# Cross-attention with 32 batches on one core: the context's values with channels stationary and 512 tokens moving, and a new order of fill and end

## The chip, the cores and the metric

One core of a Trainium2 chip runs the whole kernel. The metric is the time of one execution on the device in microseconds (us), lower is better. A core has five engines with an instruction queue each: TensorE (PE in the profile; its weight loads have a row of their own, PEld), VectorE (DVE), ScalarE (ACT), GpSimd (POOL) and SyncE (SP). SP issues all DMA transfers of this kernel, in order, and 16 DMA engines carry them out. Each engine works through its own queue in order, and semaphores make it wait for the others.

## The reference

```python
# x: (32, 512, 640) f32; ctx: (32, 77, 1024) f32; 20 heads of 32 channels
q = heads(x @ to_q_w)                       # to_q_w: 640 x 640
h_txt = sdpa(q, heads(ctx @ to_k_w), heads(ctx @ to_v_w))   # 1024 x 640 each
# the "object", "others" and "ip" parts attend to slices [77:81], [81:85], [85:] of the
# context, which has 77 rows: these slices are empty and add nothing
out = merge(h_txt) @ to_out_w + to_out_b + x
# sdpa(q, k, v) = softmax(q @ k.T / sqrt(32)) @ v, per batch and head
```

Everything is in float32. The kernel keeps that precision by splitting an operand into a high part that TensorE can take and a low part, the difference, and by adding three products (high x high, high x low, low x high: the list PAIRS).

## The kernel before, in words

**Fill.** The 32 x 77 = 2464 rows of the context are treated as one list of tokens, cut into five groups (GROUPS_KV): four of 512 and one of 416. For each group `context` (L139) loads the rows on SP, transposes them on VectorE so that channels lie on partitions, and `split` (L103: the high part by a copy on ACT, the low part by a subtraction on VectorE) makes the eight tiles `ct` (nine buffers). `keys` (L167) multiplies them with the key weights for five blocks j of 128 channels (keys stationary on the weight side, 512 tokens moving, 24 matmuls a block) and stores the split result `ks` to the scratch tensor k_dram. `context_values` (L191) does the values the other way round: 128 tokens of the context are stationary, 320 channels of the value weights (half h of 640) move. Its result is already [tokens, channels]; it is split into `vs` and stored, 640 KB and one DMA for 128 tokens, to v_dram, laid out [token, head, channel, high/low]. Group 0 also loads and splits the key weights (wk, inside `context`) and then the value weights (wv); group 1 is followed by the query weights (wq) and group 2 by the output weights, which are split and parked in wo_dram. `kvc` holds three buffers of raw context (`cs`). In the last group x of batch 0 is loaded, transposed and split.

Up to L289 the order of instructions on each engine comes from a planner: a program order serves as priority, and the planner simulates when each instruction could start. After that, under `manual_schedule`, each engine's order is the program's.

**Slots.** The main part has N = 160 slots, one for each batch b and channel block j (four heads each). `slot(n)` (L568) contains: `scores(n, t)` for the four blocks t of 128 queries (PE, then a maximum on VectorE), `exps` (ACT), the queries of slot n + 1 (`queries`, PE; `split_q`, ACT and VectorE), and the softmax of slot n - 1: `sums` (VectorE), `normalize` (POOL), `transpose_p` (32 x 32 transposes on VectorE, then four stores to a scratch tensor `pd`), and the load back as `raw` (`load_p`). Three slots later (LAG = 3) `cast_p` (ACT), `rest_p` (ACT and VectorE) and `last_p` (POOL) split these probabilities into `pp`, and `values` (PE) and `split_a` follow (`take` is both). `piece` issues the output projection of an earlier batch in portions of four steps (12 matmuls of 320 columns); `finish` adds the projection to the residual `xr` on VectorE, which frees the `po` bank, and stores a finished block of 128 rows. There are three po banks. A slot has output pieces from n = 7 on (`has_out`). `refill` reloads keys and values of the next batch from k_dram and v_dram (`load_keys`, `load_values`).

**Between fill and slots.** The values of the last group are computed in the manual part, as eight halves on a pool of three PSUM banks (`psv`): four ahead of slot 0, two in slot 0 and two in slot 1. Then the pools of the fill are released, `load_p(0)` follows, and the split output weights come back from wo_dram in five loads of 640 KB: two after slot 2, two after slot 3, one after slot 4.

**End.** `end` (L638) completes slots 157 to 159 and the output of the last two batches.

## Time and profile before

| | |
|---|---|
| median of 3 runs | 1980.47 us (1978.42 to 1981.48) |
| profiled execution: time / span | 1980.38 / 1978.6 us |
| mean granted TensorE clock | 0.991 |
| busy: PE, PEld | 1946.0 us (98%), 1761.7 us (89%) |
| busy: ACT, DVE, POOL | 1595.6 us (81%), 1345.8 us (68%), 986.0 us (50%) |
| DMA queue of SP | 555,789 packets, 421.1 MB, 83.8% of 16 engines |

The span goes from the first to the last instruction; the profiled execution's own time is 1.8 us longer. Busy shares are averages over fill, slots and end, which have different limits; a stage is to be read on its own. "PE" counts a matmul as busy from its issue to its modelled end, so matmuls overlap and a mean duration is longer than the distance from one to the next. A wait is put down to the semaphore that came last.

### The profile page before, as it was taken

What the parts mean: (1) busy time and instruction counts of PE and PEld (TensorE: products, weight loads), DVE (VectorE), ACT (ScalarE), POOL (GpSimd) and SP (SyncE); (2) the same over time, 40 slices, a digit from 0 to 9 for tenths busy, and PEclk for the clock granted to TensorE, in tenths of its full rate; (3) what the DMA queues carried; (4) which work ended last, traced back from release to release, by engine and by line L of the source; (5) the groups of instructions that cost most, each with busy time, mean ns of one, the idle gap of its engine ahead of it and who ended that gap; (6) DMA issues with size and microseconds to landing.
All of it is one profiled execution on the core that took longest, in us unless ns stands there. A gap on an engine that the chain in (4) does not pass through costs nothing.

```text
span 1978.6 us, 38192 instructions
## 1 busy us (share of the span) xinstructions
PE 1946.0 (98%) x11012; PEld 1761.7 (89%) x11012; DVE 1345.8 (68%) x2156; ACT 1595.6 (81%) x6377; POOL 986.0 (50%) x620
## 2 busy tenths in 40 slices
PE   9999998999999999999999999999999999999998
PEld 7889996799999999999999999999999999999997
DVE  4443235777777777777777777777777777777763
ACT  3322137899999999999999999999999999999982
POOL 0000033566555555565555666655665556655644
PEclk9999999899999999999999999999999999999999
DMA  7994368888889898889888988888888888888975
GB/s 170 217 263 120 96 146 206 212 220 228 228 220 229 224 225 230 225 231 225 228 223 225 226 229 221 234 223 228 226 227 226 225 224 219 225 228 225 231 195 156
DMA packets 555996, 423.54 MB, mean 214 GB/s; under 512 B 170191, under 2 KB 459501, under 8 KB 555789
## 3 DMA queue, kind: packets, MB, share of 16 engines
q1 hardware_dynamic: 555789, 421.10, 83.8%
q8 instruction: 91, 1.49, 0.3%
q14 instruction: 116, 0.95, 0.2%
HBM read 245.61 MB, written 175.32 MB: 213 GB/s over the span
## 4 chain that ended last, share of the span: by engine, by line
PE 90%; DMA 4%; SPq 2%; ACT 1%; DVE 1%; issue 1%; POOL 1%; DVEq 0%; ACTq 0%; POOLq 0%
PE po L503 28%; PE pq L346 28%; PE pa L473 15%; PE sc L381 10%; PE pv L200 4%; PE pk L171 4%; DMA raw<-pd 1%; SPq L114 1%; DMA k_dram<-ks 1%; SPq L155 1%; DMA v_dram<-vs 1%; DMA wraw<-in_L_xattn_to_k_w_dram 0%; POOL pn L414 0%; DMA wraw<-in_L_xattn_to_out_w_dram 0%; DMA cs<-in_ctx_dram 0%
## 5 line engine op out<-in xcount | busy, mean ns | idle before, releaser
L399 ACT ACTIVATE pn<-sc,nm 128x77 f32<-128x77 f32 x2560 | 797.6, 328 | 44.6 <-DVE nm L389 31.1
L414 POOL TENSOR_TENSOR pn<-pn,rs 128x1232 f32<-128x1232 f32 x160 | 364.3, 2277 | 670.2 <-DVE rs L409 655.4
L503 PE MATMUL po<-wo_s,at 128*128 128x320 f32 x3840 | 626.9, 312 | 3.0 <-DVE xr L531 3.0
L346 PE MATMUL pq<-xt,wq_s 128*128 128x512 f32 x2400 | 621.0, 399 | 0.0
L503 PEld LDWEIGHTS po<-wo_s,at 128*128 128x128 f32 x3840 | 566.3, 189 | 3.6 <-DVE xr L531 3.2
L399 ACT ACTIVATION_READ_ACCUMULATOR pn<-sc,nm 128x1 f32 x2560 | 529.3, 207 | 0.0
L389 DVE TENSOR_REDUCE nm<-sc 128x4 f32<-128x308 f32 x640 | 294.5, 460 | 335.0 <-PE sc L381 330.6
L346 PEld LDWEIGHTS pq<-xt,wq_s 128*128 128x128 f32 x2400 | 430.4, 190 | 76.7
L473 PE MATMUL pa<-pp,vb 128*128 128x512 f32 x1280 | 331.2, 400 | 13.0 <-POOL pp L459 11.0
L238 POOL TENSOR_TENSOR xt<-xs,xt 128x512 fp32r<-128x512 f32 x160 | 203.9, 1292 | 269.2 <-ACT xt L237 262.0
L473 PEld LDWEIGHTS pa<-pp,vb 128*128 128x128 f32 x1280 | 243.3, 197 | 53.7 <-POOL pp L459 13.5
L421 DVE STREAM_TRANSPOSE z<-pn 128x1280 f32<-128x1280 f32 x160 | 241.0, 1506 | 21.4 <-POOL pn L414 19.7
L452 DVE TENSOR_TENSOR pp<-raw,pp 128x1024 fp32r<-128x1024 f32 x160 | 196.2, 1226 | 59.5 <-ACT pp L445 52.8
L381 PEld LDWEIGHTS sc<-kc,qt 128*128 128x128 f32 x1280 | 213.0, 190 | 23.6 <-issue 2.1
L381 PE MATMUL sc<-kc,qt 128*128 128x154 f32 x1280 | 223.1, 256 | 2.4 <-DVE qt L363 2.3
L459 POOL TENSOR_TENSOR pp<-raw,pp 64x512 fp32r<-64x512 f32 x160 | 208.7, 1305 | 27.0 <-ACT pp L451 14.6
L363 DVE TENSOR_TENSOR qt<-pq,qt 64x512 fp32r<-64x512 f32 x320 | 214.2, 669 | 6.9 <-ACT qt L357 2.5
L496 POOL TENSOR_TENSOR xr<-xr,bias 128x640 f32<-128x640 f32 x128 | 200.8, 1570 | 9.7
L361 ACT CAST qt<-qt 64x512 fp32r<-64x512 f32 x320 | 198.1, 619 | 9.0
L381 PE MATMUL sc<-kb,qt 128*128 128x308 f32 x640 | 195.9, 306 | 0.0
L445 ACT CAST pp<-raw 128x1024 fp32r<-128x1024 f32 x160 | 170.1, 1063 | 9.3 <-DMA raw<-pd 9.2
L104 ACT CAST at<-pa 128x512 fp32r<-128x512 f32 x160 | 94.5, 591 | 94.8 <-PE pa L473 94.7
(40 smaller groups left out, 1528.5 us busy)
## 6 DMA issues: line engine op xcount, KB each, us to landing
pd<-z SPq DMA_DIRECT2D x640, 160.0 KB, 3.5
raw<-pd SPq DMA_DIRECT2D x160, 512.0 KB, 4.5
xs<-in_x_dram SPq DMA_DIRECT2D x128, 320.0 KB, 6.1
xr<-in_x_dram SPq DMA_DIRECT2D x128, 320.0 KB, 3.9
out_dram<-xr SPq DMA_DIRECT2D x128, 320.0 KB, 3.0
raw<-pd SPq DMA_DIRECT2D x160, 128.0 KB, 4.4
v_dram<-vs SPq DMA_DIRECT2D x19, 640.0 KB, 3.7
k_dram<-ks SPq DMA_DIRECT2D x80, 128.0 KB, 2.4
```

The costliest lines, as they stand in the source:

```text
L238: low.tensor_tensor(parts[1], src, parts[0].bitcast(F32), ALU.subtract)
L346: nc.tensor.matmul(pqs[n], wq_s[:, k, a, j * P : (j + 1) * P], xts[b, k][:, c, :], start=(k == 0 and m == 0), stop=(k == NC_ - 1 and m == 2),)
L363: nc.vector.tensor_tensor(qt[r, 1 + w, :], pq[r], qt[r, 0, :].bitcast(F32), ALU.subtract)
L381: nc.tensor.matmul(sc[:, cols], qt[:, m, t * P : (t + 1) * P], keys_, start=(m == 0), stop=(m == 2),)
L389: nc.vector.tensor_reduce(nm, sc[:, :KCOLS].rearrange("p (h k) -> p h k", k=NKEY), AX.X, ALU.max, negate=True)
L399: nc.scalar.activation(pnb[n % 2][:, at, :NKEY], sc[:, i * NKEY : (i + 1) * NKEY], AF.Exp, bias=nm[:, i : i + 1], accum_out=sms[n][:, at : ...
L414: nc.gpsimd.tensor_tensor(pf, pf, rs.unsqueeze(2).to_broadcast([P, NQ * HPC, NKEY]), ALU.mult)
L421: nc.vector.transpose(z.rearrange("p b t j -> p t b j"), pn.rearrange("p (t h) k -> p t (h k)", t=NQ).rearrange("p t (b i) -> p t b i", i=Q),)
L459: nc.gpsimd.tensor_tensor(pp[64:, 4, :], raw[:64, 2, :], pp[:64, 4, :].bitcast(F32), ALU.subtract)
L473: nc.tensor.matmul(pas[n], vb[:, t, :, a], pp[:, c, :], start=(m == 0), stop=(m == len(PASSES) - 1),)
L496: nc.gpsimd.tensor_tensor(xrs[b, t], xrs[b, t], bias, ALU.add)
L503: nc.tensor.matmul(pos[b, t, h][:, :HALF], ats[b * NC_ + j][:, a, t * P : (t + 1) * P], wos[0][:, j, c, h * HALF : (h + 1) * HALF], start= ...
```

## The change

1. **Values of the context.** `context_values(g0, gn, j, pool)` now works on a block j of 128 channels: the value weights are stationary, the group's tokens (512 or 416) move, 24 matmuls a block. The result is [channels, tokens]; VectorE transposes it in 32 x 32 blocks out of PSUM into `vt`, it is split from there into `vs`, and four DMAs (one for each of the four heads of the block) store it. v_dram is laid out [token, head in block, block, channel, high/low], so that one store writes pieces of 256 bytes, and `load_values` reads pieces of two or three blocks.
2. **Context a group ahead.** Loading is a function of its own, `load_context`; the loads of group g + 1 are written after the split of group g and ahead of its keys. The store of zeros comes after the first group's loads, and a context load ahead of the key weights of the same k.
3. **Keys.** Groups 0 to 3 run k outside and j inside; only the last group has j outside.
4. **Last group's values.** Five blocks in place of eight halves: two ahead of slot 0, one in slot 0, two in slot 1.
5. **Slots without output pieces (n < 7).** `last_p` comes ahead of `normalize`; `transpose_p` comes after `split_q` and `exps(n, 2)`; `scores(n, 3)` comes ahead of `values`. The five loads of the output weights follow slots 2 to 6, one each.
6. **Last slot and end.** In slot 159 both pieces come ahead of `values(156)`, and its score blocks are not held up by them. In `end`, the pieces 6 and 7 of the batch before come with a `finish` each ahead of `transpose_p(159)`; the last batch's output blocks are closed two by two with the start of the last one between; the very last block is stored in two halves.

```diff
-    v_dram = dram.tile([NT + KPAD - NKEY, HEADS, HD, 2], FPR, name="v_dram")
+    v_dram = dram.tile([NT + KPAD - NKEY, HPC, NC_, HD, 2], FPR, name="v_dram")
...
+    def load_context(g0, gn, k0, kn):
         src = ehs_flat[g0 : g0 + gn, :].rearrange("(a j) (q u) -> q j a u", j=Q, q=4)
...
+        cs = kvc.tile([P, G // Q, 4 * Q], F32, tag="cs", name="cs", bufs=3)
+        for q in range(4):
+            nc.sync.dma_start(
+                cs[q * Q : (q + 1) * Q, : gn // Q, : kn * Q],
+                src[q, :, :, k0 * Q : (k0 + kn) * Q],
+            )
+        for k in range(kn):
+            css[g0, k0 + k] = cs[:, : gn // Q, k * Q : (k + 1) * Q]
+
+    def context(g0, gn, k):
+        raw = kvt.tile([P, G], F32, tag="craw", name="craw")
+        nc.vector.transpose(
+            raw[:, :gn].rearrange("p (a j) -> p a j", j=Q), css.pop((g0, k))
+        )
+        ct = kvp.tile([P, 2, G], FPR, tag="ct", name="ct", bufs=9)
+        split(ct[:, 0, :gn], ct[:, 1, :gn], raw[:, :gn])
+        cts.append(ct)
...
+    def context_values(g0, gn, j, pool):
+        na = gn // Q
         pv = pool.tile([P, G], F32, tag="ps", name="pv")
         for k in range(NK):
             for n, (a, c) in enumerate(PAIRS):
                 nc.tensor.matmul(
-                    pv[:tn, :HALF],
-                    cts[k][:, a, t0 : t0 + tn],
-                    wv_s[:, k, c, h * HALF : (h + 1) * HALF],
+                    pv[:, :gn],
+                    wv_s[:, k, a, j * P : (j + 1) * P],
+                    cts[k][:, c, :gn],
                     start=(k == 0 and n == 0),
                     stop=(k == NK - 1 and n == 2),
                 )
...
+        vt = kvp.tile([P, G], F32, tag="vt", name="vt", bufs=1)
+        nc.vector.transpose(vt[:, :gn], pv[:, :gn])
+        vs = kvp.tile([P, G // Q, HD, 2], FPR, tag="vs", name="vs", bufs=2)
+        split(vs[:, :na, :, 0], vs[:, :na, :, 1], vt[:, :gn].rearrange("p (a d) -> p a d", d=HD))
+        dst = v_dram[g0 : g0 + gn, :, j].rearrange("(a t) i d c -> i t a (d c)", t=Q)
+        for i in range(HPC):
             nc.sync.dma_start(
-                v_dram[g0 + t0 : g0 + t0 + tn].rearrange("p h d a -> p (h d a)").bitcast(F32),
-                vs[:tn].rearrange("p h d a -> p (h d a)").bitcast(F32),
+                dst[i].bitcast(F32),
+                vs[i * Q : (i + 1) * Q, :na].rearrange("p a d c -> p a (d c)").bitcast(F32),
             )
...
-    for g0, gn in GROUPS_KV:
-        context(g0, gn)
-        if g0 == GROUPS_KV[-1][0]:
+    g0, gn = GROUPS_KV[0]
+    starts = {0: 1, 1: 1, 2: 2, 4: 4}
+    for k in range(NK):
+        if k in starts:
+            load_context(g0, gn, k, starts[k])
+        split_weights(wk_s[:, k], wk, k)
+        context(g0, gn, k)
...
+    for g, (g0, gn) in enumerate(GROUPS_KV):
+        if g:
+            cts.clear()
+            for k in range(NK):
+                context(g0, gn, k)
+        if g + 1 < len(GROUPS_KV):
+            for k0 in range(0, NK, 4):
+                load_context(*GROUPS_KV[g + 1], k0, 4)
+        else:
...
-        if g0 == 0:
+        if g + 1 < len(GROUPS_KV):
             for k in range(NK):
                 for j in range(NC_):
                     keys(g0, gn, j, k)
...
-            for t0 in range(0, gn, P):
-                for h in range(2):
-                    context_values(g0, gn, t0, h, psk)
+            for j in range(NC_):
+                context_values(g0, gn, j, psk)
...
-        v = v_dram.rearrange("n (j i) d a -> n j i (d a)", i=HPC)
+        v = v_dram.rearrange("n i j d a -> n j i (d a)")
...
-            if h == 1:
+            if (b, t) == (B - 1, NQ - 1):
+                nc.sync.dma_start(out[b, t * P : (t + 1) * P, cols], xr[:, cols])
+            elif h == 1:
                 nc.sync.dma_start(out[b, t * P : (t + 1) * P, :], xr)
...
+        rs = sums(n - 1) if n else None
+        if taken is not None and not has_out:
+            last_p(taken)
         if n:
-            normalize(n - 1, sums(n - 1))
-        if taken is not None:
+            normalize(n - 1, rs)
+        if taken is not None and has_out:
             last_p(taken)
...
         s = scores(n, 2)
-        if n:
+        if not ahead:
+            exps(n, 2, *s)
+            piece(bo_, first)
+            s = scores(n, 3)
+        if n and has_out:
             transpose_p(n - 1)
         if ahead:
             split_q(n + 1)
-        exps(n, 2, *s)
+            exps(n, 2, *s)
+        if n and not has_out:
+            transpose_p(n - 1)
...
+        if not ahead:
+            exps(n, 3, *s)
+            finish()
+            piece(bo_, first + 1)
+            take(taken)
+            return
         if has_out:
             piece(bo_, first)
+        else:
+            s = scores(n, 3)
         if taken is not None:
             values(taken)
...
-        s = scores(n, 3)
+        if has_out:
+            s = scores(n, 3)
...
         normalize(N - 1, sums(N - 1))
-        transpose_p(N - 1)
-        finish()
         add_bias(last - 1, 3)
         piece(last - 1, 6)
+        finish()
         piece(last - 1, 7)
         finish()
+        transpose_p(N - 1)
         load_p(N - 1)
...
         begin(6, 0, 4)
+        close(0)
+        close(1)
+        begin(7, 0, 4)
+        close(2)
+        close(3)
...
-        for half in halves[:2]:
-            context_values(*half, psv)
+        context_values(g0, gn, 0, psv)
...
-        for half in halves[2:4]:
-            context_values(*half, psv)
-        for n in range(LATE):
-            slot(n, halves[4 + 2 * n : 6 + 2 * n])
+        context_values(g0, gn, 1, psv)
+        slot(0, ((g0, gn, 2),))
+        slot(1, ((g0, gn, 3), (g0, gn, 4)))
...
+        for n in range(LATE, N):
             slot(n)
-            for k in {LATE: (0, 1), LATE + 1: (2, 3), LATE + 2: (4,)}.get(n, ()):
+            if n < LATE + NC_:
+                k = n - LATE
                 nc.sync.dma_start(wos[0][:, k].bitcast(F32), wo_dram[:, k].bitcast(F32))
```

## The prediction

> **What bounds the kernel now.** I read the table by stage first, cut where the matmul stream changes its kind (0 to 267 us: keys and values of the context, groups 0 to 4; 267 to 361: slots 0 to 6; then the steady slots; from 1929 the end).
>
> ```profile
> core 0: us, PE busy (x) PEld busy (x) DVE busy (x) ACT busy (x) POOL busy (x), PEclk, DMA share, GB/s
> ...
> 8.80:39.80 31.00, 29.50 (x120) 23.57 (x121) 18.93 (x28) 12.84 (x20) 0.00 (x0) 0.94 0.80 177
> 39.80:68.20 28.40, 28.39 (x194) 28.09 (x192) 6.02 (x9) 5.12 (x8) 0.00 (x0) 1.00 0.89 186
> 68.20:99.80 31.60, 29.55 (x120) 23.59 (x121) 20.75 (x35) 15.30 (x28) 0.00 (x0) 0.95 1.02 244
> 99.80:128.00 28.20, 28.20 (x194) 28.18 (x193) 6.97 (x11) 6.05 (x11) 0.00 (x0) 1.00 0.93 262
> 128.00:160.80 32.80, 29.22 (x122) 23.66 (x122) 15.24 (x25) 9.08 (x17) 0.00 (x0) 0.95 0.90 220
> ...
> 267.00:361.40 94.40, 81.18 (x428) 69.43 (x428) 47.34 (x77) 63.81 (x266) 32.81 (x22) 0.93 0.76 184
> 361.40:1929.30 1567.90, 1567.73 (x8970) 1422.08 (x8970) 1176.71 (x1882) 1443.77 (x5934) 925.81 (x576) 1.00 0.88 225
> 1929.30:1978.60 49.30, 40.55 (x238) 37.96 (x236) 18.85 (x31) 13.54 (x46) 20.29 (x12) 0.93 0.53 155
> ```
>
> The reader is to see that PE is full for 1567.7 of the 1567.9 steady us (152 slots of 10.3), and that the diff leaves those slots' instructions as they are. All that can change lies in three places where PE has holes: key groups that take 31.0, 31.6 and 32.8 us, slots 0 to 6, and the end. Next, the chain that ended last gives the price of a full group:
>
> ```profile
> 132.64 28.20 PE pk L171 x116
> 160.84 28.16 PE pv L200 x192
> 189.00 27.23 PE pk L171 x120
> 216.22 28.16 PE pv L200 x192
> 244.38 22.61 PE pk L171 x120
> ```
>
> A 512-wide matmul costs 28.2/120 = 235 ns, a 320-wide one 28.16/192 = 147, a 416-wide one 22.61/120 = 188: 0.46 ns a column, whatever the width. Last, the waits, in the window of slots 0 to 7 and then in that of the end (PE's only):
>
> ```profile
> PE pa L473 <- POOL pp L459: 8.8, 4, 2.5
> ...
> ACT pp L445 <- DMA raw<-pd: 6.1, 2, 3.2
> ```
> ```profile
> PE po L503 <- DVE xr L531: 3.0, 1, 3.0
> PE pa L473 <- POOL pp L459: 2.0, 1, 2.0
> ```
>
> **The change part by part.** I sum against the profiled execution: 1980.38 us, span 1978.6, 1.8 around it. The median of the three runs, 1980.47, is the same to 0.1, so no correction is made.
>
> *Values with 512 tokens moving.* Groups 0 to 3: before 192 x 147 ns = 28.2 us, after 5 tiles x 24 x 235 = 28.2. Nothing. Group 4 has 416 tokens; its last block of 32 tokens cost as much PE as one of 128. Before 28.2, after 120 x 188 = 22.6: 5.5 us less PE. Two tiles (9.0) stand ahead of slot 0 where four halves (14.1) stood, so slot 0 could start 12.6 us after queries(0) (266.8) and not 17.5. But its scores need load_keys(0, 0), whose last DMA is issued at 278.2 behind the key stores and, at the row's 2.8 us to landing, arrives at 281: 14.2 after. So 3.3 there; slots 0 and 1 hold 13.6 us of values for 14.1: 0.5. load_p(0) takes memory that the value buffers leave and may eat some. Booked: -3.5, bounds -5.5 and -1.
>
> *The eviction.* Per tile VectorE gains a transpose (nearest row: 128x512 from SBUF 700 ns; from PSUM not in the trace) and ACT and VectorE split 512 wide (591 to 620 and 688) instead of 320 wide (449 and 484). Per group VectorE goes from 8 x 0.48 = 3.9 to 5 x 1.4 = 7 us, ACT from 3.6 to 3.1. Cover: the 28.2 us of value matmuls, in which VectorE is busy for 6 to 7. If a transpose cost twice as much, 10 of 28: still covered. Nothing.
>
> *The stores.* One DMA of 640 KB with 5120-byte rows per block becomes four of 128 KB per tile, 256 bytes a piece: 20 issues a group for 4. At 0.45 us each SP spends 7 us more a group, past key stores and context loads; a group lasts 56 us and about 48 issues fill 24 of it. Hidden. The transfer is the doubtful part. By the trace's packet records a 5120-byte packet takes 217 ns, so a group's 512 take 512 x 217 / 16 engines = 7 us. Afterwards 10,240 pieces. No store that small is in the trace; 256-byte reads (vb) take 18.8 ns, and 512-byte packets 32 (steady) to 49 (39.8 to 130 us). So 12 us a group at 19 ns, 31 at 49. The Trainium skill, "DMA: Bandwidth & Descriptors", Specifications, speaks against the change: below 512 bytes the engine does a read-modify-write and misses line rate. Read as a piece costing two passes, 2 x 18.8 = 38 ns, an estimate from that page and the vb row: 24 us. I take 25 ns (16 us, 9 more than now), nearest to the vb row, for on the read side halving the packet nearly halves its time. From 160 us on the DMA share is 0.26 to 0.66, room for any of these; from 39.8 to 160.8 it is 0.89 to 1.02, with no room. There the stores push back loads of wv, context and weights.
>
> *Values read back.* vb<-v_dram pieces grow to 512 and 768 bytes: 61,440 packets become 24,576. At 18.8 ns now and 32 to 50 then, 10 us of 16 engines over the whole run, under a full PE. Nothing.
>
> *Context a group ahead, keys k by k.* Holes against 28.2: 31.6 and 32.8 us, so 8.0 in groups 1 and 2. The first is the context load (cs issued at 58.4, landed at 68.4); loading it before keys(0) removes it. The second is ACT, which copies wo in its queue and waits up to 3.6 us for each wo_dram store, the context split behind it. Keys k by k need a split every 3.5 us instead of eight in 5.6, so a late split hurts less, but that ACT queue stays. Against it: eight context loads (2 MB, 4.1 us of SP issue, 9 us of 16 engines) move ahead of wv in SP's queue. Now the fifth wv block is ready at 41.3 us and the sixth at 56.7, behind twenty key stores; matmuls interleaved over the tiles eat a block in 3.5 us from 39.9, so the sixth is needed at 57.4. One block fewer ahead of the key stores means a wait of 2 to 5.5 us. The store of zeros leaves the head of SP's queue (0.47 us) and context now goes ahead of the wk blocks there: within 0.5 us either way, at nothing. Also x(0) goes out behind the last stores of group 3 (issued at 246.6, split ended at 265.9, queries(0) at 266.8): no slack, 0 to 3 lost. Booked: -8 + 4 + 2 = -2; bounds -8, and +15 where the small pieces clog the queue.
>
> *Slots 3 to 6.* last_p now runs on POOL ahead of normalize (2.28 us), which removes the four PE waits; but ACT is the bound there. Its cast_p starts at 317.6, 328.0, 341.0, 353.5, 363.4: intervals of 10.4, 13.0, 12.5, 9.9. The excess is the two waits for raw (6.1 in sum). The load issued at 331.6 took 9.3 us, behind two 640 KB wo_s blocks; these now go one to a slot. What is late next: normalize comes 1.3 us later and transpose_p stands behind split_q on VectorE (1.4), so pd is stored 2 to 3 us later and its load comes nearer to the next wait. Booked -2.5, bounds -5 and +2.
>
> *The end.* take(156) moves behind another 12 output matmuls, past the 2.0 us wait for POOL. finish moves ahead of transpose_p(159), which waited on VectorE for POOL until 1944.5 and held po banks: the 3.0 us hole goes. From 1946.4 the next 4.4 us ran at clock 0.50. Here the Trainium skill ("TensorE: Matmul & The Clock Gate", Part 1) says that the clock halves after an idle window of about 3.4 us; by that a 3.0 us hole costs itself alone and the gain is 5.0. The row says that the half clock came too, and lasted into 1950.8 to 1955.1 (0.80): some 3 us more, 8 in all. New instead: values(158) needs raw(158), whose store still starts at 1935.9 and whose load lands near 1946; after cast_p, rest_p and last_p that is 1949.4, while PE arrives at 47: some 2 us of hole. transpose_p(159), itself freed from the late normalize, ends near 1944; its store and load (3.5 and 4.5 us to landing) are in by 1954 and split by 1957, and values(159) come after 60 output matmuls at 1958.7: covered by 1.5 us. So -6, bounds -4 and -7.5. The last store in two halves gives 0.3 at most.
>
> Sum: -3.5 - 2 - 2.5 - 6 = -14: 1980.4 - 14 = 1966.4 us.
>
> **The rivals.**
> (a) Everything works: both fill holes go (-8), -5.5 ahead of the slots, -5 in slots 3 to 6, -7 at the end: -25.5, 1955. For it: each hole has an order as its cause, and the diff changes that order. Against it: DMA at 0.89 to 1.02 just where more is asked of it.
> (b) Slower: small stores clog the one DMA queue between 40 and 160 us. ACT, in order, waits for a vs buffer (two of them) whose four stores have not landed, and the context split stands behind it. At 49 ns the two groups stored there ask 2 x (31 - 7) = 48 us of 16 engines from a stretch that has none. Half of it, 24 us, is absorbed by the slack after 160 us and the buffers, the rest stops PE: +24, against -12 from the end and the slots: +12, 1992. It decides from the point where the fill loses more than 12 us, near 37 ns a piece.
> (c) The change doesn't do what it says in the fill: its order comes from a planner on simulated times, wv comes late by 5 us, the second hole stays, and of the slots only 1 is won. With -6 at the end: -3.5 + 5 - 1 - 4 = about -3.5, 1977.
>
> **How the numbers follow.** Forecast 0.50, (a) 0.25, (b) 0.13, (c) 0.12. 0.2% is 4 us, about what a measurement of this kernel can tell from no change: faster means under 1976.5. The forecast's own bounds run from 1957 to 1976. Range: from below (a) for its uncertainty, 1951, to 1983, which takes in (c) and cuts most of (b). Faster: all of (a), 0.48 of the forecast and a little of (c), 0.77; same 0.09; slower 0.14.
>
> **What would show it.** Right: key groups 1 and 2 near 28 to 30 us; queries(0) to the first scores 14 to 15 us and not 17.5; intervals of cast_p near 10.5 to 11.5 in slots 4 to 6; no 3 us hole and no half clock after 1930, from the last slot's scores (1929.3 now) to the end 43 us and not 49; steady slots at 10.3. Wrong: value groups of over 28.2, ACT waiting for v_dram<-vs, packets of 256 bytes at 40 ns, or a steady slot that isn't 10.3.

## The result, and the profile after

| | before | changed | ratio |
|---|---|---|---|
| median, first comparison | 1978.42 us (7 runs) | 1971.86 us (7 runs, 1969.15 to 1974.74) | 0.9963 [0.9951, 0.9974] |
| median, on another chip (run `again`, below) | 1979.13 us (9 runs) | 1972.59 us (5 runs, 1969.72 to 1974.12) | 0.9965 [0.9951, 0.9978] |
| profiled execution | 1980.38 us, span 1978.6 | 1974.74 us, span 1972.9 (slowest of its seven); again: 1972.59, span 1970.7 | |

The change is 6.6 us faster, so 7.4 us of the 14 booked were not won. (The time itself is 5.5 above the 1966.4 forecast, for before ran 2 us faster here than in its profile.) Where they went is read from six marks on the time axis: the first weight load of queries(0), the cast_p of slots 3, 8, 13 and 158 (ScalarE, tile pp, one per slot), and the span's end. Each number is a difference of two starts in the trace.

| stretch, us | before | after | again | booked | measured |
|---|---|---|---|---|---|
| start to queries(0): fill | 266.6 | 268.6 | 268.7 | -2 | +2.0, +2.0 |
| to cast_p of slot 3 | 50.9 | 48.2 | 48.1 | -3.5 | -2.7, -2.9 |
| to cast_p of slot 8 | 56.3 | 55.4 | 53.2 | -2.5 | -0.9, -3.1 |
| to cast_p of slot 13 | 51.5 | 55.7 | 52.4 | 0 | +4.2, +0.9 |
| to cast_p of slot 158 | 1493.8 | 1493.3 | 1496.6 | 0 | -0.4, +2.8 |
| to the end | 59.4 | 51.6 | 51.8 | -6 | -7.8, -7.7 |

Two terms missed: the fill lost 2 us instead of winning 2, and the steady slots, booked at nothing, lost some 3.7 us in both profiles (rows four and five added). The end won more than booked. Before has a single profile; how far such stretches differ from one execution to the next is told under `again`.

The table by stage of the changed kernel, cut where its matmul stream changes: keys 0 and the hole after them; values 0, keys 1 and values 1; keys 2; up to queries(0); slots 0 to 6; steady slots; the end from the last slot's first scores.

```profile
core 0: us, PE busy (x) PEld busy (x) DVE busy (x) ACT busy (x) POOL busy (x), PEclk, DMA share, GB/s
7.56:43.69 36.13, 28.40 (x121) 22.21 (x121) 18.37 (x27) 10.62 (x17) 0.00 (x0) 0.97 0.94 189
43.69:127.55 83.86, 83.86 (x361) 69.24 (x361) 38.55 (x56) 27.82 (x44) 0.00 (x0) 0.97 0.89 202
127.55:164.70 37.15, 30.32 (x121) 24.22 (x120) 17.02 (x26) 9.77 (x16) 0.00 (x0) 0.86 0.88 205
164.70:268.80 104.10, 104.10 (x482) 89.99 (x481) 40.03 (x64) 23.90 (x42) 4.49 (x4) 1.00 0.68 135
268.80:362.00 93.20, 80.20 (x375) 68.88 (x375) 52.70 (x84) 65.25 (x273) 37.41 (x25) 0.93 0.81 182
362.00:1931.44 1569.44, 1565.06 (x8952) 1418.97 (x8951) 1174.67 (x1878) 1440.80 (x5924) 925.52 (x576) 1.00 0.87 225
1931.44:1972.90 41.46, 37.66 (x238) 35.61 (x236) 18.77 (x31) 13.65 (x46) 20.36 (x12) 1.00 0.61 186
```

The end is 41.5 us for 49.3, at clock 1.00 for 0.93. The fill has two stretches with idle PE: 36.1 us with 28.4 of work, and 37.2 with 30.3, the latter at clock 0.86. Which engine PE waits for there is in the waits, first PE's in 20 to 145 us, then ScalarE's in 85 to 145 (engine, tile and line, what it waited for: us in all, times, longest):

```profile
PE pk L163 <- ACT ct L104: 6.7, 1, 6.7
PE pv L190 <- ACT wv_s L104: 5.2, 1, 5.2
```
```profile
ACT vs L104 <- DMA v_dram<-vs: 10.0, 3, 6.3
ACT wscaled L119 <- DMA wraw<-in_L_xattn_to_q_w_dram: 9.5, 3, 8.3
ACT ws L104 <- DMA wraw<-in_L_xattn_to_out_w_dram: 8.5, 1, 8.5
ACT ws L104 <- DMA wo_dram<-ws: 5.8, 2, 4.8
```

The lengths of holes given from here on run from the end of the last weight load ahead of a hole to the start of the next, some 0.4 us more than the wait in such a line. The first hole (38.0 to 43.7, 5.7 us) waits for wv: the loads of group 1's context stand ahead of wv in SP's queue. The second (130.7 to 137.8, 7.1 us, ahead of group 2's second block of context) waits for a context split on ScalarE, which had been waiting for three things: the value stores, and the loads of wq and wo and the store of wo. Behind each hole the clock is low for a while (0.57 on the mean in 41 to 49 us and again in 133 to 145): of the 10.0 us by which keys 2 are longer than a full group without a hole, 27.2 us, the hole is 7.1 and the clock 2.9. In ScalarE's order these stand just ahead of the late split (start, duration, what it waited for):

```profile
131.10 0.65 ACT L104 CAST vs<-vt 128x512 fp32r<-128x512 f32 x1 [6.34 <-DMA v_dram<-vs]
136.50 0.72 ACT L104 CAST ws<-wraw 128x640 fp32r<-128x640 f32 x1 [4.75 <-DMA wo_dram<-ws]
137.13 0.61 ACT L104 CAST ct<-craw 128x512 fp32r<-128x512 f32 x1
```

A split of wo comes last, behind the store of the one before it. What the time would be with one of these gone, the lines don't say. That is what most of the runs are for. PE's chain in the end, in the window from 1931.44:

```profile
1936.80 1.87 PE pa L475 x8
1938.67 5.28 PE po L505 x36
1943.95 1.88 PE pa L475 x8
1945.83 3.51 PE po L505 x24
1949.34 2.06 PE pa L475 x8
1951.40 8.78 PE po L505 x60
1960.18 1.88 PE pa L475 x8
1962.06 4.06 PE po L505 x28
```

From 1936.8 to 1966.1 each piece begins where the one before ends: no hole at all.

### The profile page after: what moved, and what is told of

The parts are those of the page before. It is cut to its first block, busy times and chain, and to the rows that moved or that the text cites. A ratio compares the mean times of both kernels' runs of the same rounds, so it can differ in the third digit from the quotient of the medians.

```text
span 1972.9 us, 37606 instructions
## 1 busy us (share of the span) xinstructions
PE 1935.1 (98%) x10652; PEld 1732.9 (88%) x10652; DVE 1362.0 (69%) x2166; ACT 1594.4 (81%) x6362; POOL 988.0 (50%) x620
## 4 chain that ended last, share of the span: by engine, by line
PE 88%; DMA 4%; SPq 3%; DVE 2%; ACT 1%; issue 1%; POOL 0%; ACTq 0%; DVEq 0%; POOLq 0%
PE po L505 28%; PE pq L348 27%; PE pa L475 14%; PE sc L383 10%; PE pv L190 5%; PE pk L163 4%; DMA raw<-pd 1%; SPq L114 1%; SPq L143 1%; SPq L203 1%; ACT pn L401 0%; DMA wraw<-in_L_xattn_to_k_w_dram 0%; DMA wraw<-in_L_xattn_to_q_w_dram 0%; DMA k_dram<-ks 0%; DMA pd<-z 0%
```

## The experiments

The theory from the traces: the end's new order is worth its 7.8 us, slots 0 to 2 some 3; the fill gives back 2, by an order in SP's queue (first hole) and by what stands in ScalarE's queue (second hole). The rival for the fill is that its first 130 us are bound by bytes, so that a closed hole opens again later. Times are set against before, run on the same chip; the changed kernel itself is at -6.6 and -6.5.

| run | edit to the changed kernel | median | against before | ratio |
|---|---|---|---|---|
| wv_first | context 1 behind wv | 1962.82 | -15.0 | 0.9930 [0.9918, 0.9942] |
| vs3 | third vs buffer | 1971.45 | -6.4 | 0.9969 [0.9957, 0.9981] |
| wo_later | wo in group 3 | 1969.71 | -8.1 | 0.9955 [0.9944, 0.9967] |
| all3 | these three | 1968.61 | -9.2 | 0.9956 [0.9944, 0.9968] |
| old_end | old end | 1975.76 | -2.7 | 0.9988 [0.9979, 0.9996] |
| old_slots | old slots 0 to 6 | 1971.60 | -6.8 | 0.9967 [0.9955, 0.9979] |
| old_values | old values | 1982.44 | +4.0 | 1.0018 [1.0009, 1.0026] |
| pool_w | wv_first, wq and wo on GpSimd | 1966.05 | -12.4 | 0.9928 [0.9916, 0.9940] |
| wo_raw | wo unsplit, in the slots | 1960.63 | -18.9 | 0.9901 [0.9886, 0.9916] |
| wv_wo_raw | wv_first and wo_raw | 1958.58 | -20.9 | 0.9893 [0.9879, 0.9906] |
| wv_wo_ct | that, and context splits on GpSimd | 1966.94 | -12.5 | 0.9936 [0.9923, 0.9948] |

### wv_first: the first hole

```
 for g, (g0, gn) in enumerate(GROUPS_KV):
...
-        if g + 1 < len(GROUPS_KV):
+        if 0 < g < len(GROUPS_KV) - 1:
             for k0 in range(0, NK, 4):
                 load_context(*GROUPS_KV[g + 1], k0, 4)
-        else:
+        elif g:
...
             for k in range(NK):
                 split_weights(wv_s[:, k], wv, k)
+            for k0 in range(0, NK, 4):
+                load_context(*GROUPS_KV[g + 1], k0, 4)
```

> The changed kernel with one step moved back: the loads of group 1's context are issued behind the eight blocks of wv (and not ahead of them); everything else as changed. Theory (the loss of the fill is an order in SP's queue): the 5.2 us hole ahead of the first value matmul (PE waits for wv, at 38.4) closes to under 1 us, and the keys of group 1 start without a hole of over 1.5 us since they are needed only at about 66; queries(0) at 264 to 266 instead of 268.8, ratio to the changed kernel 0.998 or below. Rival (the first 130 us are bound by the bytes that the DMA engines move, whose share is 0.88 to 0.95 there): the hole only moves to the keys of group 1 and is 3 to 5 us again, queries(0) at 268 to 270, no difference beyond 1 us.

1962.8 us, 8 to 9 below the changed kernel. queries(0) starts at 261.3 (268.6). PE's waits in 36 to 145 us:

```profile
PE pk L163 <- ACT ct L104: 3.5, 1, 3.5
PE pv L190 <- ACT wv_s L104: 1.2, 1, 1.2
PE pk L163 <- DVE ct L105: 0.8, 1, 0.8
```

The wait for wv falls from 5.2 to 1.2, and keys 1 take 27.2 us, as long as any full group without a hole: nothing opens again at 66 us. So the rival (bytes) falls for this place, although the DMA share in 8.8 to 130 us is 0.93: what counts is which bytes go first. The second hole shrinks too, to 4.0 and 1.3 us: PE comes to it 6.3 us earlier, but the late context split starts 9.4 us earlier (127.7 for 137.1), since the planner now has it ahead of that split of wo. A new hole of 1.6 us stands ahead of queries(0).

### vs3, wo_later, all3: the second hole, first attempt

vs3:

```
-            scaled = kvw.tile([P, C], F32, tag="wscaled", name="wscaled", bufs=1)
-            nc.scalar.mul(scaled, raw, scale)
-            raw = scaled
+            nc.scalar.mul(raw, raw, scale)
...
-        vs = kvp.tile([P, G // Q, HD, 2], FPR, tag="vs", name="vs", bufs=2)
+        third = pool is psk and (g0 // G * NC_ + j) % 3 == 2
+        vs = (kvt if third else kvp).tile(
+            [P, G // Q, HD, 2], FPR, tag="vs", name="vs", bufs=1 if third else 2
+        )
```

> The changed kernel with a third buffer for the split values (vs) in the groups 0 to 3, for which wq is scaled in place; everything else as changed. Theory (ScalarE, whose queue is in order, waits for the small value stores, and the splits of the next context stand behind it): ScalarE's waits for v_dram<-vs in 90 to 140 us fall from 10.0 us to under 4, and the hole in the keys of group 2 from 6.7 us to 3 or 4; total 2 to 3.5 us less. Rival 1 (the chain of wo, whose single buffer waits for its own store, holds ScalarE): the waits for vs fall and the hole stays within 1 us of 6.7. Rival 2 (DMA bandwidth): the same, and the wait moves to ct or wo.

wo_later:

```
-        if g0 == GROUPS_KV[2][0]:
+        if g0 == GROUPS_KV[3][0]:
             for k in range(NC_):
                 ws = kvw.tile([P, 2, C], FPR, tag="ws", name="ws", bufs=1)
```

> The changed kernel with the splitting of wo and its five stores moved from group 2 to group 3; everything else as changed. Theory (the loads, splits and stores of wo stand in ScalarE's queue ahead of group 2's context splits): the hole in the keys of group 2 falls from 6.7 us to under 3, 3 to 5 us less at queries(0), unless the same chain now makes x(0) late there, which would show as a hole ahead of queries(0). Rival (the small value stores and the two vs buffers alone hold ScalarE): the hole stays within 1 us of 6.7 and the total within 1 us.

all3 has both of these edits and that of wv_first.

> The three edits together: group 1's context behind wv, a third buffer for the split values, wo in group 3. Theory (the holes of the fill come from orders and buffers): both holes under 1.5 us, no half clock in the fill after 20 us, queries(0) at about 268.8 - 5 - 6 = 258 to 260, total 8 to 11 us below the changed kernel (1961 to 1964). Rival (bytes in the first 130 us): at most 3 us below it.

A third buffer takes ScalarE's waits for v_dram<-vs in that window from 10.0 us to under 1, and the hole is still 5.0 (7.1): the waits went to the loads of wq (11.5) and the stores of wo (10.7), and the split of wo ahead of the context split now waits 9.5 us for its store and starts at 135.7 us (136.5). The place of the waits is what the first rival says, the hole lies between it and the theory, and the time is that of the changed kernel. wo_later did not do what it says: ScalarE splits wo at 112.3, 120.0, 135.2 us, where the changed kernel does at 112.6, 120.6, 136.5, because the planner of the fill moves work by readiness and not by its place in the text. So it says nothing of its theory: its hole is 5.5 us, and the 1.5 us by which it is ahead of the changed kernel are within what executions of one kernel differ by (`again`). all3 is a miss: the first hole is gone as in wv_first, but the second is 9.7 us, and it is 6 us slower than wv_first alone. In its trace the context split is behind a split of wo again, which waits 8.2 us for a store and starts at 132.8; the two other edits weren't tried one by one on wv_first.

### pool_w and wo_raw: the second hole, second attempt

pool_w is wv_first with this edit in split_weights (the scaling of wq is on GpSimd too):

```
+        if scale is not None or not permuted:
+            nc.gpsimd.tensor_copy(dst[:, 0, :], raw)
+            nc.gpsimd.tensor_tensor(dst[:, 1, :], raw, dst[:, 0, :].bitcast(F32), ALU.subtract)
+        else:
             split(dst[:, 0, :], dst[:, 1, :], raw)
```

> The kernel with group 1's context loads behind wv, and besides all splits of wq and wo on GpSimd, which does nothing in the fill; everything else as in that one (1962.8). Theory (the hole in the keys of group 2, 5.3 us in two parts there, is ScalarE's in-order queue, in which wq and wo stand waiting for their loads and stores ahead of the context): ScalarE's waits for wscaled and ws are gone and the hole falls below 2 us, total 3 to 5 us less, 1958 to 1960. Rival 1 (the two vs buffers alone): within 1 us of 1962.8. Rival 2 (GpSimd is slow at these operations, keeps the wraw buffers and delays wo): up to 4 us slower.

wo_raw is the changed kernel without wo in the fill:

```
-        if g0 == GROUPS_KV[2][0]:
-            for k in range(NC_):
-                ws = kvw.tile([P, 2, C], FPR, tag="ws", name="ws", bufs=1)
-                split_weights(ws, wo, k, permuted=False)
-                nc.sync.dma_start(wo_dram[:, k].bitcast(F32), ws.bitcast(F32))
...
             slot(n)
+            if 0 <= n - LATE - 1 < NC_:
+                k = n - LATE - 1
+                hi, lo = (wos[0][:, k, i] for i in range(2))
+                nc.vector.tensor_copy(hi, raw_wo[k])
+                nc.gpsimd.tensor_tensor(lo, raw_wo[k], hi.bitcast(F32), ALU.subtract)
             if n < LATE + NC_:
                 k = n - LATE
-                nc.sync.dma_start(wos[0][:, k].bitcast(F32), wo_dram[:, k].bitcast(F32))
+                raw_wo.append(late[0].tile([P, C], F32, tag="xr", name="xr", bufs=3))
+                nc.sync.dma_start(raw_wo[k], wo[k * P : (k + 1) * P, :])
```

> The changed kernel, but wo is neither split in group 2 nor stored: its five blocks of 320 KB are loaded unsplit in slots 2 to 6 (where five split blocks of 640 KB are loaded now) and split there, the high part on VectorE and the low part on GpSimd. Theory (in slots 3 to 8 the wait for raw is made by the bytes that the one queue moves, the DMA engines being 0.9 busy there, and not by the order of the slots): from the first cast_p to that of slot 8 it takes 52 to 53.5 us instead of 55.4, and with wo's loads, splits and 3.2 MB of stores out of the fill the hole in the keys of group 2 falls from 7.1 us to 3 to 5; total 3 to 6 us below the changed kernel. Rival for the slots (raw waits for its own chain of store and load): 55 +- 1 us there. Rival for the fill (the two vs buffers alone make the hole): 7 us still.

pool_w takes wq and wo out of ScalarE's queue and keeps their loads and stores. It runs in 1966.1 us (1961.3 to 1967.4), 12.4 below before where wv_first is 15.0 below: the theory's 1958 to 1960 is missed. The hole stays (3.6 and 1.3 us; 4.0 and 1.3 in wv_first). ScalarE's waits in 85 to 145 us, then what it does around the context split:

```profile
ACT vs L104 <- DMA v_dram<-vs: 26.3, 6, 7.5
ACT ks L104 <- DMA k_dram<-ks: 16.2, 3, 11.7
```
```profile
126.66 0.65 ACT L104 CAST vs<-vt 128x512 fp32r<-128x512 f32 x1 [5.51 <-DMA v_dram<-vs]
127.20 0.61 ACT L104 CAST ct<-craw 128x512 fp32r<-128x512 f32 x1
```

The time that ScalarE no longer spends on wo, it spends waiting for the stores of values and keys. So my theory falls for what is left of the hole in wv_first: there the split already stands behind a split of values (127.7), as it does here (127.2), and not behind wo. In the changed kernel, where a split of wo is the last ahead of it, moving wo's splits alone wasn't tried. wo_raw takes out the traffic as well, and in the changed kernel: 1.6 MB of loads and 3.2 MB of stores on the one queue, and SP's own waits for the splits that it stores. PE's waits in 36 to 145 us of wo_raw, then ScalarE's in 85 to 145, then what it does around the context split:

```profile
PE pv L189 <- ACT wv_s L103: 5.4, 1, 5.4
```
```profile
ACT vs L103 <- DMA v_dram<-vs: 11.8, 4, 7.1
ACT ks L103 <- DMA k_dram<-ks: 11.4, 2, 9.4
```
```profile
128.08 0.65 ACT L103 CAST vs<-vt 128x512 fp32r<-128x512 f32 x1 [7.11 <-DMA v_dram<-vs]
128.63 0.61 ACT L103 CAST ct<-craw 128x512 fp32r<-128x512 f32 x1
```

The second hole is gone altogether: keys 2 take 27.2 us for 37.2. The context split starts 8.5 us earlier than in the changed kernel. ScalarE's waits for the value stores are no shorter (11.8 for 10.0), and the split still stands behind one, but PE, which starts keys 2 at 128.1, needs it only at 131.5. So wo holds the hole of the changed kernel open. Whether it does so by its splits in ScalarE's queue, by its bytes (in 85 to 127.5 us the queue moves 189 GB/s for the changed kernel's 222, at a share of 0.90 for 0.92) or by SP standing in its queue for wo's splits isn't separated. The wait for the value stores is the next thing in line: in wv_first PE needs the same split at 124.7, before that wait is over, and the hole of 4.0 us is the result.

In the slots the waits are as the theory has them: ScalarE waits for raw for 1.4 us in 300 to 375 us, for 6.1 and 4.2 in the two profiles of the changed kernel, with half the bytes for wo. A gain in time isn't shown. From cast_p of slot 3 to that of slot 8 it takes 52.7 us, but the nine profiles that have the new order and load wo split lie between 51.6 (old_end) and 55.7 (vs3). The total, 11 to 12 us below the changed kernel, is twice the most that was expected, since the whole hole went, and the low clock behind it.

### wv_wo_raw and wv_wo_ct: both together

> wo loaded unsplit in the slots, and group 1's context loads behind wv: the two edits together. Theory (the two losses are separate: the first hole is SP's order, the second is work in ScalarE's queue and the store traffic): the sum of both gains, 1971.9 - 9 - 3 to 6 = 1957 to 1960, with the first hole under 2 us and the second under 4. Rival (one queue's bytes tie them together, so that a gain in one place is given back in the next): 1961 to 1964, no better than wv alone (1962.8).

> As the one before, and the context splits of groups 1 to 4 on GpSimd, which has an empty queue in the fill, instead of ScalarE and VectorE. Theory (the second hole is the context split standing in the in-order queues of ScalarE and VectorE behind the split values that wait for a buffer): the waits for vs stay and the hole in the keys of group 2 falls below 1.5 us, total 2 to 4 us below the kernel with the two edits. Rival (the context itself is late, or GpSimd's two operations a block, some 2.5 us, are too slow for keys that need a block every 3.4 us): hole of 3 us or more, or keys of groups 1 to 3 that last over 28.5 us.

wv_wo_raw runs in 1958.6 us (1957.89 to 1959.56), the fastest of all: 13 to 14 us below the changed kernel and 21 below before. queries(0) is at 256.0. PE's waits in 36 to 145 us:

```profile
PE pv L189 <- ACT wv_s L103: 2.0, 1, 2.0
PE pk L162 <- DVE ct L104: 1.1, 1, 1.1
```

This is in the theory's range and below the rival's. The gains still don't add (8.4 and 12.3 below the changed kernel give 14.3, all against before), for both edits bring the same context split forward: from 137.1 us to 127.7 with the one, to 128.6 with the other, to 126.2 with both. Besides, values 0 take 31.1 us here for 28.6 in wv_first, with the wait for wv a little longer. That a gain is given back is what the rival says; why it is, no run shows.

In wv_wo_ct GpSimd splits the context (a 128x512 copy in 0.61 us, a subtraction in 1.33). The fill is 0.5 us shorter, queries(0) at 255.5, and then 7.5 us are lost up to the cast_p of slot 3 (55.6 us for 48.1), 4.5 of them up to the first scores, which come 18.5 us after queries(0) and not 14.0. In 255 to 275 us:

```profile
ACT ks L103 <- DMA k_dram<-ks: 5.3, 3, 2.2
PE sc L385 <- DMA kb<-k_dram: 4.6, 1, 4.6
```

The last keys are stored and read back later. The hole that it was to close was closed (two smaller ones, 1.3 and 1.4 us, opened at 67.8 and 85.9, where PE waits for GpSimd's splits), and the next thing in order became late. Neither theory had that.

### old_end, old_slots, old_values: what each part is worth

The end and the last slot as before (values(156) first, transpose_p(159) ahead of finish), the rest changed:

```
-        if not ahead:
-            exps(n, 3, *s)
-            finish()
-            piece(bo_, first + 1)
-            take(taken)
-            return
...
         normalize(N - 1, sums(N - 1))
+        transpose_p(N - 1)
+        finish()
         add_bias(last - 1, 3)
         piece(last - 1, 6)
-        finish()
         piece(last - 1, 7)
         finish()
-        transpose_p(N - 1)
         load_p(N - 1)
...
```

> The changed kernel with the last slot and the end as they were before the change (values(156) first, transpose_p(159) ahead of finish, the last store whole); fill and slots as changed. Theory (the end's order is worth what its stretch shows, 49.3 us before and 41.5 after): total 7 to 8 us above the changed kernel, a 3 us hole of PE and a half clock of some 6.8 us are back in the end, and nothing earlier than the last slot differs. Rival (part of the 7.8 is the execution: the profiled run of the changed kernel is the slowest of its seven): 4 to 6 us. The stall of slots 10 to 12 in the changed kernel's profile, 3.8 us, should not be in this profile if it belongs to the execution, and should be if it belongs to the order.

From cast_p of slot 158 to the end 58.2 us, where the changed kernel has 51.6 and 51.8: 6.5. The median is 3.9 higher, and by the differences to before 2.7 and 6.6 also 3.9, at the edge of the rival's 4 to 6; the 6.5 of the traces is nearer to the theory. In the profiles what makes up for the rest lies in slots 3 to 12, which the edit leaves alone: 103.9 us for 111.1 and 105.6. PE's waits in the end are the two of before again:

```profile
PE po L505 <- DVE xr L533: 3.0, 1, 3.0
PE pa L475 <- POOL pp L461: 2.0, 1, 2.0
```

and after the 3.2 us hole (1941.62 to 1944.86) PE runs slow (PEclk is the number behind the PE column):

```profile
1938.00:1944.86 6.86, 3.89 (x27) 1.00 0.61 173
1944.86:1948.20 3.34, 3.34 (x12) 0.73 0.85 174
1948.20:1952.50 4.30, 4.30 (x26) 0.81 0.61 195
```

Next, the order inside slots 0 to 6 as before (wo's loads stay at one a slot):

```
-        if taken is not None and not has_out:
-            last_p(taken)
         if n:
             normalize(n - 1, rs)
-        if taken is not None and has_out:
+        if taken is not None:
             last_p(taken)
...
+        if n:
+            transpose_p(n - 1)
         if ahead:
             split_q(n + 1)
...
```

> The changed kernel with the order inside slots 0 to 6 as before (last_p behind normalize, transpose_p ahead of split_q, the fourth scores behind the values); the loads of wo stay one to a slot. Theory (in slots 3 to 8 the wait for raw is the bound, and the new order only moves it): from the first cast_p to that of slot 8 it takes 55.4 +- 1 us as in the changed kernel, total within 1.5 us of it. Rival (the new order is worth what was booked for it): 3 us more in these slots, with the waits of values for last_p (8.8 us in sum before the change) back.

1971.6 us, 6.8 below before where the changed kernel is 6.6 below: no difference, as far as intervals of 2.4 us to either side can tell. From cast_p of slot 3 to that of slot 8 54.5 us, between the two profiles of the changed kernel. PE's longest wait in 300 to 385 us, first in old_slots, then in the changed kernel:

```profile
PE pa L475 <- POOL pp L461: 6.4, 3, 2.5
```
```profile
PE sc L383 <- ACT pn L401: 8.0, 3, 4.9
```

The new order takes away the waits of values for last_p, and PE then waits as long for score banks that ScalarE has not read yet. A wait of PE was moved, and no gain is seen.

Last, the values as before, tokens stationary and stored in 5120-byte rows, everything else changed (both forms are in the diff of the change).

> The changed kernel with the values made as before (tokens stationary, 320 channels moving, 5120-byte rows stored) in groups 0 to 4, with their old places in slots 0 and 1; the order of the fill, of the slots and of the end stays changed. Theory (the values' new form gains 0.9 us in each of the groups 0 to 3 and 5.5 in group 4, and its small stores cost little): queries(0) 2 to 4 us later, from it to the first cast_p 1.5 to 3 us longer, total 4 to 7 us above the changed kernel. Rival (the 256-byte stores, behind which ScalarE waits for a buffer, make the hole in the keys of group 2): that hole falls from 6.7 us to under 3, queries(0) is no later than 268.8, total +3 or less.

1982.4 us, 10.6 above the changed kernel and slower than before: more than the theory said, and far from the rival's 3 or less. queries(0) is at 276.5, 7.9 later. PE's waits in 36 to 145 us:

```profile
PE pv L192 <- ACT wv_s L104: 10.9, 2, 5.7
PE pk L163 <- DVE vs L105: 3.1, 1, 3.1
```

The second hole is gone (keys 2 take 27.2 us), but not by the larger stores: PE comes to keys 2 15.8 us later than in the changed kernel, and the late split, behind a split of wo as there, starts only at 143.9. And there are two waits for wv, at 38 and at 57 us, the sixth block of wv being the one behind the key stores; the changed kernel has only the first, since its planner puts 36 matmuls of group 1's keys behind the first 45 of the values. From one group's first matmul to the next group's, value groups last 28.2 us in the old form and 27.2 in the new.

### again: which part of a profile belongs to the execution

> The changed kernel itself once more, on another chip. Theory (the 4 us that slots 8 to 13 lost in its first profile belong to that execution, an unlucky meeting of a load of raw with the loads of x, and not to the change): from the cast_p of slot 8 to that of slot 13 it takes 51.5 to 52.5 us and not 55.7, while the two holes of the fill (5.7 and 7.1 us) and the 51.6 us of the end are the same within 1 us; profiled time near 1970. Rival (the change's order of the slots makes that stall): 55 us again.

The holes of the fill are the same within 1 us (6.6 and 7.0 us), the end is (51.8), and slots 8 to 13 take 52.4 us for 55.7: most of that stall belonged to that execution. But the later slots lose 2.8 us against before instead, at slots 15, 20, 25, 30 and others: about half of the fifth slots, those after the loads of x, have an interval of 10.9 to 12.4 us and the next one of 9.5. ScalarE's waits for raw in 370 to 1925 us, before and in `again`:

```profile
ACT pp L445 <- DMA raw<-pd: 3.2, 4, 1.5
```
```profile
ACT pp L447 <- DMA raw<-pd: 20.3, 18, 2.1
```

In the first profile of the changed kernel it is 4.6, in the other eleven kernels 4.8 to 15.3. Before has the least, but only one profile, so whether the change brings some of it stays open. The spread speaks for executions: from the cast_p of slot 8 to that of slot 158, a stretch that no edit touches, the eleven other kernels take 1545.5 to 1550.1 us, both profiles of the changed kernel 1549.0 and before 1545.3. The fill has such a spread too. In old_slots, which leaves it as changed, queries(0) starts at 266.1 us and the second hole is 5.6. So a size of 2 to 4 us from one profile is that of one execution.

## Why the prediction was right, and where it was not

The direction and the range are right, and so is the mechanism of the end. Of the sum less than half came, 6.6 of 14, and it was luck that a miss of 4 us in the fill was in part made up by 1.8 us more at the end. By its own steps:

- **The end, -6: it was -7.8.** The 3.0 us hole and the half clock went as said, and old_end has both back. The term that was too large is the 2 us hole ahead of values(158). cast_p(158) starts at 1947.1, 1.0 earlier than the estimate with the 2.1 us by which the whole end comes later. PE starts values(158) at 1949.3 without a hole, although last_p(158) ends only at 1950.6: the eight matmuls take 2.06 us for 1.88. So the other bound, -7.5, was the nearer value.
- **The clock.** The rule of the Trainium skill ("TensorE: Matmul & The Clock Gate", Part 1), an idle window of about 3.4 us, would have the half clock missing after the hole of before; the row said otherwise. old_end shows it again after a hole of 3.2 us, 4.8 us after the hole's start; and in the changed kernel's profile it comes after one of 2.8 us at 410.3, from 413.5 on. Summing by the row was right; what the rows of this case have in common is in the last section.
- **Values ahead of slot 0, -3.5: it was -2.7 and -2.9.** The first scores come 14.0 us after queries(0), where 14.2 was worked out and before had 17.5.
- **A full value group, booked at nothing: it won 1.0 us.** The price of 235 ns for a 512-wide matmul was taken from 28.20 us, a row that has 116 matmuls, not 120, and a slow clock (0.95 in 128.00 to 160.80). The row 27.23 for 120 of the same matmuls stood two lines below: 227 ns. The 320-wide ones cost 28.16/192 = 147 ns, so the price of a column is not the same at every width: 0.458 ns against 0.443. From start to start the traces have 146.7 ns at 320 columns, 186.6 at 416 and 226.7 at 512, which is 13.3 ns a matmul and 0.417 ns a column. Over four groups that is 4 us that the fill should have had besides.
- **The fill, -2: it was +2, and without the mis-sized values +6.** The wait for wv was booked at +4, at the sixth block of wv; the hole was 5.7 us, at the first block, and the low clock behind it was booked at nothing. The step that failed is "Holes against 28.2: ... so 8.0 in groups 1 and 2", booked whole. Of the second hole the same paragraph says that its ACT queue stays, and its 4 us were counted as won all the same; keys 2 went from 32.6 to 37.2 us. wo_raw shows that wo holds it, which the change leaves where it was; by which of its loads, splits and stores is open. The first of the two, keys 1 at 31.6, did go. x(0), booked at +2, was in time.
- **The stores.** 256 bytes take 22.1 ns on the mean in 40 to 130 us and 22.5 in 130 to 285 by the trace's packet records (30,512 of them there), against 25 booked from the row of the 256-byte reads and 38 by the read-modify-write of the Trainium skill ("DMA: Bandwidth & Descriptors", Specifications). The row was the better guide. Rival (b) decided from 37 ns on, and is out. The chain that it names is there, though: ScalarE waits for a vs buffer with the context split behind it, and in wv_first that makes a hole of 4.0 us.
- **Values read back.** Wrong, and without effect: 58,752 packets of 256 bytes at 18.4 ns are left in 370 to 1970 us, not 24,576 larger ones. The pieces are contiguous in v_dram now, but not in vb.
- **Slots 3 to 6, -2.5: -0.9 and -3.1.** The size is in the bounds, the mechanism only half right: the waits for last_p went, and no gain from the order inside the slots is seen (old_slots). One interval of 13.5 and 13.0 us is left where 10.5 to 11.5 were forecast. What made the stretch shorter isn't shown: with one load of wo a slot it takes 51.6 to 55.7 us in nine profiles, with the old order 54.5.
- **Steady slots, booked at nothing: some +3.7 in both profiles**, in the first by the stall of slots 8 to 13, in the second mostly by waits for raw at fifth slots. This is the other part of what is missing, and whether the change brings it is open, as said above.
- **Rival (a)**, everything works, is what wv_wo_raw comes near to, with an order and a transfer changed that the change didn't touch: 1958.6 for 1955. **Rival (c)** had the fill right in kind, wv late and the second hole there, and the end too small: its text says -6 there and its sum has -4 (with -6 it gives 1975, not 1977).

## What to carry to other kernels

When a load is moved ahead, name the transfer that it now stands in front of: the queue's order decides even where the engines are 0.9 busy, and moving the eight loads of a context behind the eight blocks of wv was worth more here (8.4 us) than the whole change (6.6). If a hole is caused by a chain that the change leaves in place, don't book the hole as won. A wait that is seen on an engine is a symptom: ScalarE's waits for the small stores were as long without the hole as with it. What counts is what stands just ahead of the late instruction in its engine's order, and when the next engine needs it. Test a cause in the kernel that has it: pool_w moved wo's splits in a kernel where another wait had already taken their place.

## What the runs showed of the hardware that was not expected

- A hole of PE of 2.8 to 3.2 us can be followed by the half clock, which sets in after PE has resumed (in old_end the hole ends at 1944.86, the half clock begins at 1946.4). In each of the fourteen profiles the times at which the clock changes lie 3.41 us, or a multiple of it, apart. From the first full clock on, a fall to half came only at the end of such a stretch in which PE was busy for at most 0.59 of the time, always where it was busy for under 0.45, and in some cases between. So PE need not be idle for the whole of it. Near the end of the kernel before, PE is busy for 1.15 us of 3.41 (first line), and in the next stretch the clock is at half although PE works:

```profile
1942.29:1945.70 3.41, 1.15 (x8) 1.00 0.58 193
1945.70:1949.11 3.41, 2.69 (x8) 0.50 0.63 125
```

- The stretch ahead of the half clock has 1.52 us of PE in old_end (to 1946.38) and 1.01 in the changed kernel (to 413.50).
- Storing 256-byte pieces costs 22.1 to 22.5 ns each on the mean in the fill, reading such pieces 18.4 in 370 to 1970 us and 20.5 in the first 40 us. The median is 18 in all of these stretches of the changed kernel, so most of the difference is in the stretch and not in the direction.
- Making the memory side of a transfer contiguous (v_dram, for the loads of vb) left its packets at 256 bytes. The rows on the other side, in vb, are that short; that they are the reason is argued and wasn't tried.
